# Products with a feature table for a few tiles per chunk, in a four-layer graph network on one core

## The chip, the cores and the metric

The kernel runs on one core of a Trainium2 chip. A core has five engines that run their own instruction streams side by side: TensorE (PE: matrix products, results in PSUM), VectorE (DVE), ScalarE (ACT), GpSimd (POOL) and SyncE (SP, which here only issues transfers). Sixteen DMA engines move data between memory and SBUF. The metric is the device time of one execution in microseconds (us), lower is better. Before the change the median of 14 runs is 22,172.26 us (22,068.88 to 22,297.55).

## What is computed

A graph of 12,500 nodes with 32 features and 400,000 edges sorted by target goes through four pre-norm residual layers. Each layer takes `h = relu(layernorm(x))`, makes a message per edge from the source's row (layer two from the target's row too) and adds the messages up at the targets. Cut to what matters here:

```python
# layer 0
m = relu(h[src] + edge_attr_32)
x = x + (1 + eps) * h + segment_sum(m, dst)
# layer 1: emb = edge_attr_10, edge_vec = edge_attr_3, norm = edge_weight
hid = sqrt(2) * relu(emb @ W1 / sqrt(10))
w = (hid @ W2 / 4).reshape(E, 7, 16, 8)
... # products of h[src], h[dst], directions and w; tanh gates
x = x + segment_sum(edge_ftr, dst)
# layer 2: rows are src, columns are dst
deg = segment_sum(ones, src); n = rsqrt(1 + deg)
xs = n * h
x = x + n * (segment_sum(xs[dst], src) + xs)
# layer 3: emb = edge_attr_8, edge_sh = edge_attr_4
hid = relu(emb @ (W1 / sqrt(8))) * sqrt(2)
w = (hid @ (W2 / 16)).reshape(E, 4, 8, 8)
... # products of h[src], edge_sh and w
x = x + segment_sum(edge_ftr, dst) / sqrt(E / N)
```

## The kernel before

Edges are cut into 196 chunks of CT = 16 tiles of 128 edges (2,048 edges a chunk); within a tile an edge is a partition. Everything is unrolled over the chunks. The stages follow one another: the first layer (`layer0`, run by `edges`), a joint pass over layers two and three (`edges12`), and the fourth layer (`edges3`). Between them `norm_relu` writes the normed features of all nodes to memory (`feats`).

**Gathers.** The rows `h[src]` come by indirect DMA on POOL, one per tile of 128 edges: L488 in the first layer, L759 in the joint pass, L1184 in the fourth. So each stage has 16 gathers a chunk, 3,136 in all.

**First layer.** Tiles go in groups of four (G = 4). `fetch` loads a chunk's indices, edge attributes and places (`load` L482 and L480, `places_of` L463; two buffers) and gathers four groups ahead, into six buffers. `main` adds the attributes (L615, DVE) and takes the relu (L616, ACT). `collect` builds a one-hot of each edge's place in its window of targets (L420, DVE, f32) and multiplies it with the messages on PE, all 16 tiles into one PSUM tile (L423, f32); the window's sum is copied (L426, ACT) and stored by SP (`put`, L448). `tail` also counts how often each node is a source: the index is split into two coordinates (L630 to L633), each becomes a one-hot (L637), and PE multiplies the two (L640, bf16). Beside all this a generator `rest` clears tables, makes weights, unit vectors and the bf16 parts of `edge_attr_8` for the fourth layer (`parts_of`, L313, 14 steps); `edges` draws from it after every second group (L563).

**Joint pass.** One pass of the loop (L993, 199 passes, 12 steps each) works on several chunks at once: the products of layer two for chunk c, its gather for c + 3, the front for c + 1, the sums for c - 1, and layer three for c - 3 and c - 4. `ends` (L773) turns the gathered rows over with 16 f32 products against the identity a chunk (L778), multiplies the window of targets with a one-hot (L782), and copies the tile X (L784, ACT). `hidden` (L794) makes the hidden layer, `product` (L801) and `reduce` (L811) the messages with an elementwise product z on DVE between them (L804). `collect` (L844) sums over targets. For layer three `lay` (L918) spreads target rows over edges, `alike` (L926) marks equal sources within a tile, `join` (L934) sums over them on PE and ACT copies the sum (L936), and `scatter` (L940) adds it to memory by an indirect DMA on POOL, 16 a chunk. PSUM tiles of the pool `ps` have one buffer.

**Fourth layer.** `edges3` multiplies hidden layer and weights in f32 (L1220) and uses a helper that the other stages don't: `thirds` (L429) writes an f32 tile as the sum of three bf16 tiles, so that a bf16 product with a one-hot keeps f32 accuracy.

## Time and profile before

| | us |
|---|---|
| median of 14 runs | 22,172.26 |
| the profiled execution | 22,128.07 |
| its span | 22,126.4 |
| first layer (first gather to the last sum stored) | about 120 to 5,140 |
| joint pass | about 5,250 to 16,500 |
| fourth layer | about 16,600 to 22,050 |
| PE busy | 14,400.2 (65%) |
| DVE busy | 11,884.2 (54%) |
| ACT busy | 5,787.4 (26%) |
| POOL busy | 14,365.1 (65%) |

Busy times are sums over the span; the stages have different limits, so each is read by itself, in a window of its own. A group of instructions in the profile is one line of the kernel, one engine and one operation: its names (written <- read), count, busy time and mean length, and then how long the engine stood idle before its instructions and what ended that. "Issue" there is time in which the engine waited for nothing that the profile shows. The column PEclk is the share of its full clock that TensorE was granted by the record. Timeline rows give the start, the length, the engine, the line and the operation.

### The profile page before, as it was taken

To read this page: it belongs to the slowest core of one execution; us is meant where nothing else is said; L and a number is where in the kernel's file an instruction comes from. 1 tells how busy PE (TensorE), PEld (TensorE's weight loads), DVE (VectorE), ACT (ScalarE), POOL (GpSimd) and SP (SyncE) were. 2 spreads that over 40 slices of the span, in tenths; PEclk is the share of its full clock that TensorE was granted. 3 is DMA by queue.
4 is the path that set the end of the run, shared out by engine and by line. 5 is a ranking of instruction groups with operands and counts; after the bars stand their busy time and mean duration, and the time that the engine had idled before them with its cause. 6 is when DMAs were issued, how large, how long until landed. Compare 5 with 4: busy or idle time off the path is not lost.

```text
span 22126.4 us, 218835 instructions
## 1 busy us (share of the span) xinstructions
PE 14400.2 (65%) x69780; PEld 8225.2 (37%) x69780; DVE 11884.2 (54%) x23464; ACT 5787.4 (26%) x13374; POOL 14365.1 (65%) x12552
## 2 busy tenths in 40 slices
PE   2333333334777777777777777777746777777776
PEld 2333333332332333333333333333325555555554
DVE  3444333334555555555555555555555666666666
ACT  0001000001222222222222222222214444444443
POOL 5666666664777777777777777777765555555554
PEclk9999999999777777777777777777768888888887
DMA  2114111112333333333333333333331111111111
GB/s 85 40 38 143 23 23 22 22 22 57 80 78 76 79 80 80 74 80 80 75 79 78 76 81 79 78 76 82 79 73 23 23 24 23 23 23 23 23 23 30
DMA packets 1528330, 1259.87 MB, mean 57 GB/s; under 512 B 1140160, under 2 KB 1303608, under 8 KB 1472776
## 3 DMA queue, kind: packets, MB, share of 16 engines
q1 hardware_dynamic: 741084, 1005.43, 14.6%
q0 software_dynamic: 752640, 206.32, 10.8%
q10 hardware_dynamic: 33430, 33.95, 0.5%
q8 instruction: 553, 9.06, 0.2%
q14 instruction: 623, 5.10, 0.1%
HBM read 1083.53 MB, written 160.90 MB: 56 GB/s over the span
## 4 chain that ended last, share of the span: by engine, by line
PE 31%; another core or an unknown queue 23%; DVE 18%; ACT 12%; issue 9%; POOL 4%; DMA 3%; DVEq 0%; ACTq 0%; SPq 0%; POOLq 0%
PE ps_y L801 11%; PE ps_o L811 5%; PE ps L934 4%; PE ps_w L1220 4%; ACT oh L836 4%; DVE z L804 3%; POOL hs L488 3%; ACT oh L765 2%; PE ps_win L423 1%; DVE pv L1228 1%; DVE pa L1224 1%; DVE f L1237 1%; PE ps_sum L844 1%; PE ps_m L778 1%
## 5 line engine op out<-in xcount | busy, mean ns | idle before, releaser
L940 POOL DMA_INDIRECT acc<-summed,rows x3136 | 4994.0, 1592 | 2052.2 <-issue 1132.9
L1184 POOL DMA_INDIRECT hs<-feat,src x3136 | 3030.8, 966 | 2455.7 <-DVE ps L1226 1457.0
L488 POOL DMA_INDIRECT hs<-feat,src x3136 | 3166.6, 1010 | 1963.1 <-issue 872.3
L759 POOL DMA_INDIRECT hs<-feat,src_c x3136 | 3172.8, 1012 | 1131.1 <-issue 936.8
L804 DVE TENSOR_TENSOR z<-ps_y,hid 128x1024 f32<-128x1024 f32 x2352 | 2843.7, 1218 | 1210.0 <-PE ps_y L801 957.8
L1220 PE MATMUL ps_w<-w2b,hid 128*128 128x256 f32 x12544 | 3208.2, 412 | 59.8 <-issue 39.9
L423 PE MATMUL ps_win<-m,oh 128*128 128x32 f32 x6272 | 1484.7, 402 | 2291.4 <-ACT m L616 1363.5
L1220 PEld LDWEIGHTS ps_w<-w2b,hid 128*128 128x128 f32 x12544 | 2593.1, 210 | 622.0 <-issue 82.7
L801 PE MATMUL ps_y<-X,w2t 64*128 64x512 f32 x4704 | 2238.0, 831 | 746.6 <-ACT hid L796 407.0
L423 PEld LDWEIGHTS ps_win<-m,oh 128*128 128x128 f32 x6272 | 1396.7, 328 | 2379.3 <-ACT m L616 1454.0
L811 PE MATMUL ps_o<-z,sums 128*32 128x512 f32 x9408 | 1924.6, 694 | 1.6 <-issue 0.8
L801 PE MATMUL ps_y<-Q,w2t 64*128 64x512 f32 x4704 | 1667.4, 733 | 79.7 <-DVE z L804 39.5
L934 PEld LDWEIGHTS ps<-hd,eq 128*128 128x128 f32 x6272 | 1044.1, 252 | 1265.0 <-issue 395.5
L934 PE MATMUL ps<-hd,eq 128*128 128x32 f32 x6272 | 1139.9, 335 | 544.5 <-DVE eq L926 189.2
L778 PE MATMUL ps_m<-eye,hs 128*32 128x128 f32 x6272 | 808.0, 369 | 1022.4 <-ACT X L784 740.1
L787 DVE TENSOR_TENSOR Q<-N,X 128x512 f32<-128x512 f32 x392 | 271.5, 693 | 2205.8 <-ACT X L784 1485.4
L1197 ACT ACTIVATE hid<-ps_h 128x1024 f32<-128x1024 f32 x784 | 800.8, 1021 | 2388.9 <-remote 1951.4
L1224 DVE TENSOR_TENSOR pa<-ps_w,q 128x512 f32<-128x512 f32 x784 | 538.4, 687 | 1648.6 <-remote 1353.5
L801 PEld LDWEIGHTS ps_y<-X,w2t 64*128 64x128 f32 x4704 | 600.3, 235 | 1795.4 <-issue 732.2
L778 PEld LDWEIGHTS ps_m<-eye,hs 128*32 128x32 f32 x6272 | 551.2, 148 | 1606.7 <-ACT X L784 866.2
L936 ACT COPY summed<-ps 128x128 f32<-128x128 f32 x784 | 207.8, 265 | 3584.5 <-PE ps L934 2368.8
L616 ACT ACTIVATE m<-m 128x128 f32<-128x128 f32 x784 | 241.9, 309 | 3417.5 <-DVE m L615 1644.4
(202 smaller groups left out, 20233.6 us busy)
## 6 DMA issues: line engine op xcount, KB each, us to landing
has<-loc_t SPq DMA_DIRECT2D x392, 1024.0 KB
srow<-in_src_t SPq DMA_DIRECT2D x392, 512.0 KB
hs<-feat,src POOLq DMA_INDIRECT x6272
N<-n_t SPq DMA_DIRECT2D x3136, 32.0 KB
emb<-pp SPq DMA_DIRECT2D x126, 448.0 KB
emb<-emb SPq DMA_DIRECT2D x196, 288.0 KB
edge_attr<-in_edge_attr SPq DMA_DIRECT2D x196, 256.0 KB
hs<-feat,src_c POOLq DMA_INDIRECT x3136
```

Of the source, the lines that this page charges most:

```text
L423: nc.tensor.matmul(c["sum"], lhsT=oh[:, k, :], rhs=feat[:, k, :], start=t0 + k == 0, stop=t0 + k == self.CT - 1)
L488: self.nc.gpsimd.indirect_dma_start(out=t[:, k, :], out_offset=None, in_=self.feats[l][:], in_offset=bass.IndirectOffsetOnAxis(ap=idx[:, t ...
L759: nc.gpsimd.indirect_dma_start(out=c["hs"][:, k, :], out_offset=None, in_=self.feats[1][:], in_offset=bass.IndirectOffsetOnAxis(ap=c["src_ ...
L778: nc.tensor.matmul(t[64 * q : 64 * q + 32, k * P : (k + 1) * P], lhsT=c["hs"][:, 4 * (2 * h + q) + k, :], rhs=self.eye, start=True, stop=True)
L801: nc.tensor.matmul(y[:, q, :], lhsT=self.w2t[64 * q : 64 * q + 64, j, :], rhs=c["Q" if j < 3 else "X"][64 * q : 64 * q + 64, h, :], start= ...
L804: nc.vector.tensor_mul(z, y, c["hid"][:, 2 * h : 2 * h + 2, :])
L811: nc.tensor.matmul(c["o", j // 3][32 * q : 32 * q + 32, :], lhsT=self.sums[:, j, :], rhs=c["z", j, q // 2][:, q % 2, :], start=j % 3 == 0, ...
L836: nc.scalar.activation(c["oh"][:, k, :], self.iota, AF.Square, bias=c["local"][:, k : k + 1], scale=-1.0)
L934: nc.tensor.matmul(t[:, k, :], lhsT=c["eq"][:, k, :], rhs=c["hd"][:, G * g + k, :], start=True, stop=True)
L940: nc.gpsimd.indirect_dma_start(out=self.tabs[2][k % NTAB][:], out_offset=bass.IndirectOffsetOnAxis(ap=c["rows"][:, G * g + k : G * g + k + ...
L1184: nc.gpsimd.indirect_dma_start(out=c["hs"][:, k, :], out_offset=None, in_=self.feats[3][:], in_offset=bass.IndirectOffsetOnAxis(ap=c["src" ...
L1220: nc.tensor.matmul(w[:, k, :], lhsT=c["hid"][:, m, 4 * g + k].rearrange("p q s -> p (q s)"), rhs=self.w2b[:, m, :], start=m == 0, stop=m == 1)
```

## The change

The last KP = 3 tiles of a chunk in the first layer, and the last KJ = 1 in the joint pass, are no longer gathered. A table of all features stands in SBUF as bf16 triples (`table`): 13 blocks of 128 rows, a row holding eight nodes, in two halves of 16 features. `codes` writes for each such edge the block, the place in the block and the node's number within the row. `found` turns these into one-hots, multiplies the table with them (13 x 2 x 3 products), keeps the one of eight nodes that is wanted, and folds the result into the tile of rows. The first three chunks (FIRST) gather all.

The first layer is written anew (`edges0`), chunk by chunk, with four buffers for loads and rows; the sums over targets go by thirds in bf16, with one-hots from ACT; the old form stays as `any0` for another kind of input that doesn't occur here. `rest` is drawn eight times a chunk, from chunk 4 on, and has more to do: `edge_attr_10` is split as `edge_attr_8` was, and each in 28 steps of half the size.

In the joint pass DVE transposes the rows (`sources`) in place of PE; the targets alone go by PE and are copied by ACT in four pieces (`targets`); the hidden layer reads the bf16 parts; the sums over targets and over equal sources go by thirds (`thirds`, `split`), the latter reduced by DVE (`joined`) where ACT copied before. Many tiles have one buffer instead of two. The fourth layer keeps its instructions.

```diff
+KP = 3
+KJ = 1
+FIRST = 3
+KB = 13
...
-        self.w1t = keep.tile([P, P], F32, name="w1tk")
-        self.w2t = keep.tile([P, 6, P], F32, name="w2t")
+        self.w1t = keep.tile([90, P], BF16, name="w1tk")
+        self.w2t = keep.tile([P, 2, 6, P], F32, name="w2t")
...
+            yield from self.parts_of(pool, self.a["ea10_c"], self.emb10)
             yield from self.parts_of(pool, self.a["ea8_c"], self.emb8)
...
-        F = flat.shape[1] // 14
+        F = flat.shape[1] // 28
...
+    def table(self, pool, l):
+        nc = self.nc
+        tab = pool.tile([P, 3, KB, 2, P], BF16, name="tab")
+        with self.tc.tile_pool(name="whole", bufs=1) as tmp:
+            x = tmp.tile([P, KB, 2 * P], F32, name="whole")
+            m = -(-self.N // 8)
+            rows = self.feats[l][: 8 * m].rearrange("(r k) d -> r (k d)", k=8)
+            n = m // P
+            nc.vector.memset(x[:, n:, :], 0.0)
+            nc.sync.dma_start(x[:, :n, :], rows[: n * P].rearrange("(b p) e -> p b e", p=P))
+            nc.sync.dma_start(x[: m - n * P, n, :], rows[n * P :])
+            for k in range(3):
+                for i in range(2):
+                    nc.scalar.copy(tab[:, k, :, i].rearrange("p b (j f) -> p b j f", f=16),
+                                   x.rearrange("p b (j i f) -> p b i j f", i=2, f=16)[:, :, i])
+                if k < 2:
+                    for i in range(2):
+                        t = x.rearrange("p b (j i f) -> p b i j f", i=2, f=16)[:, :, i]
+                        nc.vector.tensor_tensor(t, t, tab[:, k, :, i].rearrange("p b (j f) -> p b j f", f=16), op=ALU.subtract)
+        return tab
+    def edges0(self, rest):
+        nc, tc, CT, NW = self.nc, self.tc, self.CT, self.NW
+        n = KP * P
+        self.codes()
+        with ExitStack() as ctx:
+            tp = ctx.enter_context(tc.tile_pool(name="table0", bufs=1))
+            tab = self.table(tp, 0)
...
+            def fetch(c):
+                c["src"] = self.load(ld, "src", c["col"])
+                c["attr"] = self.load(ld, "edge_attr_32", c["col"])
+                c.update(self.places_of(ld, c["no"]))
+                if c["no"] >= FIRST:
+                    c["code"] = ld.tile([P, 3, n], F32, name="code", bufs=3)
+                    nc.sync.dma_start(c["code"].rearrange("p i e -> p (i e)"),
+                                      self.code[c["no"] : c["no"] + 1].rearrange("o i e -> (o i e)").partition_broadcast(P))
+                c["hs"] = ld.tile([P, CT, D], F32, name="hs")
+                for k in range(CT if c["no"] < FIRST else CT - KP):
+                    nc.gpsimd.indirect_dma_start(
+                        out=c["hs"][:, k, :], out_offset=None, in_=self.feats[0][:],
+                        in_offset=bass.IndirectOffsetOnAxis(ap=c["src"][:, k : k + 1], axis=0))
+            def found(c, step):
+                if c["no"] < FIRST:
+                    return
+                if step == 0:
+                    c["mine"] = wp.tile([P, n], BF16, name="mine")
+                    nc.vector.scalar_tensor_tensor(c["mine"], c["code"][:, 1], self.part, c["code"][:, 0],
+                                                   op0=ALU.is_equal, op1=ALU.mult)
+                    c["found"] = [pt.tile([P, n], F32, name=f"ps_half{i}") for i in range(2)]
+                elif step < 6:
+                    for b in range(3 * (step - 1), min(3 * step, KB)):
+                        oh = wp.tile([P, n], BF16, name="oh8", bufs=4)
+                        nc.vector.tensor_scalar(oh, c["mine"], float(b + 1), None, op0=ALU.is_equal)
+                        for i in range(2):
+                            for k in range(3):
+                                nc.tensor.matmul(c["found"][i], lhsT=tab[:, k, b, i], rhs=oh,
+                                                 start=(b, k) == (0, 0), stop=(b, k) == (KB - 1, 2))
+                else:
+                    own = []
+                    for i in range(2):
+                        own.append(wp.tile([P, n], F32, name=f"own{i}"))
+                        nc.vector.scalar_tensor_tensor(own[i], c["code"][:, 2], self.quad, c["found"][i],
+                                                       op0=ALU.is_equal, op1=ALU.mult)
+                    t = po.tile([P, KP, D], F32, name="ps_own")
+                    for k in range(KP):
+                        for i in range(2):
+                            nc.tensor.matmul(t[:, k, :], lhsT=own[i][:, k * P : (k + 1) * P], rhs=self.fold2[:, i],
+                                             start=i == 0, stop=i == 1)
+                    nc.scalar.copy(c["hs"][:, CT - KP :, :], t)
+            def messages(c):
+                m = c["f"] = wp.tile([P, CT, D], F32, name="m")
+                nc.vector.tensor_add(m, c["hs"], c["attr"])
+                nc.scalar.activation(m, m, AF.Relu)
+            def places(c, g):
+                oh = c["oh", g] = wp.tile([P, G, P], BF16, name="oh", bufs=2 * CG)
+                for k in range(G):
+                    t = G * g + k
+                    nc.scalar.activation(oh[:, k, :], self.iota, AF.Square, bias=c["local"][:, t : t + 1], scale=-1.0)
+                nc.scalar.activation(oh, oh, AF.Relu, bias=self.one, scale=-2.0)
+            def collect(c, g):
+                if g == 0:
+                    c["sum"] = ps.tile([P, B], F32, name="ps_sum")
+                for k in range(G * g, G * g + G):
+                    nc.tensor.matmul(c["sum"][: 3 * D, 0:P], lhsT=c["f3"][:, k].rearrange("p i f -> p (i f)"),
+                                     rhs=c["oh", g][:, k % G, :], start=k == 0, stop=k == CT - 1)
...
+            cs = [{"no": c, "col": c * CT} for c in range(NW)]
+            for c in range(2):
+                fetch(cs[c])
+            for c in range(NW + 1):
+                now, last, next_ = (cs[k] if 0 <= k < NW else None for k in (c, c - 1, c + 1))
+                if c + 2 < NW:
+                    fetch(cs[c + 2])
+                for g in range(CG):
+                    if now:
+                        if g == 0:
+                            messages(now)
+                            now["deg"] = ps.tile([P, P], F32, name="ps_deg")
+                            now["hl"] = self.coordinates(wp, now["src"])
+                        self.thirds(wp, now, g, bufs=2)
+                        places(now, g)
+                        hi, lo = now["hl"]
+                        self.degree(wp, now, hi[:, G * g : G * g + G], lo[:, G * g : G * g + G], G * g)
+                    if next_:
+                        for step in ((0, 1), (2, 3), (4, 5), (6,))[g]:
+                            found(next_, step)
+                    if last:
+                        if g < 2:
+                            collect(last, 2 * g)
+                            collect(last, 2 * g + 1)
+                        else:
+                            add(last, g - 2)
+                    for _ in range(2 if c > 3 else 0):
+                        next(rest, None)
+            for _ in rest:
+                pass
...
+            tab = self.table(ctx.enter_context(tc.tile_pool(name="table1", bufs=1)), 1)
...
-                c["emb"] = ld.tile([P, B], F32, name="emb")
-                for q in range(Q4):
-                    nc.sync.dma_start(c["emb"][32 * q : 32 * q + 10],
-                                      self.a["ea10_c"][q, :, ds(row, 1), :].rearrange("f o e -> f (o e)"))
+                c["emb"] = ld.tile([90, Q4 * B], BF16, name="emb")
+                nc.sync.dma_start(c["emb"], self.emb10[:, :, ds(row, 1), :].rearrange("k f o e -> (k f) (o e)"))
...
+                    c["src"] = gp.tile([P, CT], I32, name="src", bufs=12)
+                    nc.sync.dma_start(c["src"], self.a["src"][:, ds(c["col"], CT)])
                     c["hs"] = gp.tile([P, CT, D], F32, name="hs")
-                for k in range(G * g, G * g + G):
+                    if c["no"] >= FIRST:
+                        c["code"] = gp.tile([P, 3, KJ * P], F32, name="code", bufs=2)
+                        for i in range(3):
+                            nc.sync.dma_start(c["code"][:, i], self.code[c["no"], i, (KP - KJ) * P :].partition_broadcast(P))
+                for k in range(G * g, min(G * g + G, CT - (KJ if c["no"] >= FIRST else 0))):
                     nc.gpsimd.indirect_dma_start(
                         out=c["hs"][:, k, :], out_offset=None, in_=self.feats[1][:],
-                        in_offset=bass.IndirectOffsetOnAxis(ap=c["src_c"][:, k : k + 1], axis=0))
+                        in_offset=bass.IndirectOffsetOnAxis(ap=c["src"][:, k : k + 1], axis=0))
...
+            def found(c, s):
...
+                elif s in (1, 2):
+                    for b in ((0, 1, 2, 3, 4, 5, 6), (7, 8, 9, 10, 11, 12))[s - 1]:
+                        nc.vector.tensor_scalar(c["which"][:, b], c["mine"], float(b + 1), None, op0=ALU.is_equal)
+                if s in (2, 5):
+                    c["half"] = ps.tile([P, B], F32, name="ps_2")[:, :n]
...
+                elif s in (3, 6):
...
+                elif s == 8:
...
-            def ends(c, h):
+            def sources(c, h):
+                nc.vector.transpose(c["X"][:, h, :], c["hs"].rearrange("p t f -> p (t f)"))
+
+            def targets(c):
                 t = ps.tile([P, B], F32, name="ps_m")
-                for k in range(4):
-                    for q in range(2):
-                        nc.tensor.matmul(t[64 * q : 64 * q + 32, k * P : (k + 1) * P],
-                                         lhsT=c["hs"][:, 4 * (2 * h + q) + k, :], rhs=self.eye, start=True, stop=True)
-                for q in range(2):
-                    e0 = (2 * h + q) * B
-                    nc.tensor.matmul(t[64 * q + 32 : 64 * q + 64, :], lhsT=c["win"], rhs=c["has"][:, e0 : e0 + B],
+                for g in range(Q4):
+                    b = g ^ 1
+                    nc.tensor.matmul(t[32 * g : 32 * g + 32, :], lhsT=c["win"], rhs=c["has"][:, b * B : (b + 1) * B],
                                      start=True, stop=True)
-                nc.scalar.copy(c["X"][:, h, :], t)
+                for g in (1, 3, 0, 2):
+                    nc.scalar.copy(c["X"][32 * g : 32 * g + 32, (g ^ 1) % 2, :], t[32 * g : 32 * g + 32, :])
...
-                    r = 32 * (2 * h + q)
-                    nc.tensor.matmul(t[:, q, :], lhsT=self.w1t[r : r + 10], rhs=c["emb"][r : r + 10],
-                                     start=True, stop=True)
+                    e0 = (2 * q + h) * B
+                    nc.tensor.matmul(t[:, q, :], lhsT=self.w1t, rhs=c["emb"][:, e0 : e0 + B], start=True, stop=True)
...
-                    c["has2"] = sp.tile([P, Q4 * B], F32, name="has2")
+                    c["has2"] = sp.tile([P, Q4 * B], F32, name="has2", bufs=1)
...
+            def split(c, step):
+                if step == 0:
+                    c["hd3"] = sp.tile([P, CT, 3, D], BF16, name="hd3", bufs=1)
+                if step % 2 == 0:
+                    nc.scalar.copy(c["hd3"][:, :, step // 2, :], c["hd"])
+                elif step == 1:
+                    nc.vector.tensor_tensor(c["hd"], c["hd"], c["hd3"][:, :, 0, :], op=ALU.subtract)
+                else:
+                    nc.vector.tensor_tensor(c["hd3"][:, :, 2, :], c["hd"], c["hd3"][:, :, 1, :], op=ALU.subtract)
...
             def join(c, g):
-                t = ps.tile([P, B], F32, name="ps_2")[:, : G * D].rearrange("p (k f) -> p k f", f=D)
+                t = c["joint"] = ps.tile([P, B], F32, name="ps_2")[:, : G * 3 * D].rearrange("p (k e) -> p k e", k=G)
                 for k in range(G):
-                    nc.tensor.matmul(t[:, k, :], lhsT=c["eq"][:, k, :], rhs=c["hd"][:, G * g + k, :], start=True, stop=True)
+                    nc.tensor.matmul(t[:, k, :], lhsT=c["eq", g][:, k, :],
+                                     rhs=c["hd3"][:, G * g + k].rearrange("p i f -> p (i f)"), start=True, stop=True)
+
+            def joined(c, g):
                 c["summed", g] = sp.tile([P, G, D], F32, name="summed", bufs=2 * CG)
-                nc.scalar.copy(c["summed", g], t)
+                nc.vector.tensor_reduce(c["summed", g], c["joint"].rearrange("p k (i f) -> p k f i", i=3), AX.X, ALU.add)
...
```

## The prediction, made before the changed kernel was run

> **What bounds the kernel now.** I read the table of windows first, one row for the body of each stage: the first layer, the joint pass over the second and third layers, the fourth layer.
>
> ```profile
> core 0: us, PE busy (x) PEld busy (x) DVE busy (x) ACT busy (x) POOL busy (x), PEclk, DMA share, GB/s
> 2700.00:4900.00 2200.00, 796.36 (x4124) 755.97 (x4123) 794.40 (x2840) 119.19 (x430) 1362.92 (x1376) 1.00 0.12 22
> 5500.00:16300.00 10800.00, 8458.62 (x41536) 3312.97 (x41533) 6050.16 (x11835) 2871.56 (x6656) 7912.79 (x6076) 0.76 0.37 79
> 17000.00:21500.00 4500.00, 3240.82 (x14685) 2561.40 (x14683) 2904.03 (x3750) 2076.61 (x4564) 2523.16 (x2608) 0.84 0.12 23
> ```
>
> There are 196 chunks of 16 tiles. 1376 gathers in 2200 us are 86 chunks: 25.6 us per chunk in the first layer. The joint pass takes 11,250 us for its 199 passes of the loop, 56.5 us each, and the fourth layer some 27 us a chunk. In the first layer only POOL is more than half busy (62%); in the joint pass PE is (78%), with POOL beside it.
>
> Next the groups of instructions by line, of the window 2700 to 4900 and then of the whole span.
>
> ```profile
> L488 POOL DMA_INDIRECT hs<-feat,src x1376 | 1362.9, 990 | 829.2 <-issue 382.7 <-DVE oh L420 296.3 <-DMA src<-in_src 95.8
> ```
>
> ```profile
> L940 POOL DMA_INDIRECT acc<-summed,rows x3136 | 4994.0, 1592 | 2052.2 <-issue 1132.9
> L488 POOL DMA_INDIRECT hs<-feat,src x3136 | 3166.6, 1010 | 1963.1 <-issue 872.3
> L759 POOL DMA_INDIRECT hs<-feat,src_c x3136 | 3172.8, 1012 | 1131.1 <-issue 936.8
> ...
> L423 PE MATMUL ps_win<-m,oh 128*128 128x32 f32 x6272 | 1484.7, 402 | 2291.4 <-ACT m L616 1363.5
> ...
> L934 PE MATMUL ps<-hd,eq 128*128 128x32 f32 x6272 | 1139.9, 335 | 544.5 <-DVE eq L926 189.2
> L778 PE MATMUL ps_m<-eye,hs 128*32 128x128 f32 x6272 | 808.0, 369 | 1022.4 <-ACT X L784 740.1
> ```
>
> "Issue" on POOL is time between two of its DMAs in which it waits for nothing shown. In the first layer POOL needs (1362.9 + 382.7) / 86 = 20.3 us a chunk of its own; the other 5.3 us of the 25.6 it waits for buffers that DVE frees late. So fewer gathers help there, down to what the other engines allow. In the joint pass POOL needs (4994.0 + 1132.9 + 3172.8 + 936.8) / 196 = 52 us by this reckoning, or 49 us with the usual 1.25 us (gather) and 1.84 us (scatter) from start to start in the timeline. It then waits for sums from PE, while PE, 44 us busy a chunk, waits 740.1 us in all (3.8 us a chunk) for the copy of X before its transposes. PE's round with ACT and DVE sets the joint pass; POOL is 4 to 7 us behind it.
>
> **Clock.** The row of 2700 to 4900 says 1.00, but this is not to be trusted: L423 and L934 have one shape, and L423 costs 237 ns of PE time, L934 182. In the trace starts in L423 lie 210 ns apart; in L934 they lie either 110 or 210 apart. The 512-column bf16 product of the fourth layer (L1195) has starts 220 or 430 ns apart. I read the first layer as running at half clock, since its PE is busy 36% of the time, and price its PE work both ways.
>
> **First layer.** Removed: 3 of 16 gathers in all chunks but three. POOL: 20.3 x 13/16 = 16.5 us a chunk. Added on PE: 78 bf16 products (13 blocks x 2 halves x 3 parts) over 384 columns. From L1195, 220 x 384/512 = 165 ns or 322 ns: 12.9 us or 25.1. Six f32 products to fold the halves are 12 instructions of 110 or 210 ns: 1.3 or 2.5. The places' sums turn from 32 f32 instructions into 16 bf16 ones and the degrees stay: 32 x 60 (L1256 dense) or 110 ns, 1.9 or 3.5. PE: 16.3 us at full clock, 31.2 at half, against 9.3 now. DVE: 13 one-hots of 384 bf16 have no equal in this trace; between the small operations (150 ns) and the 128x384 f32 form (552 ns) they cost 2 to 7 us, and I take 3.5, nearer the small ones as they read and write bf16 with a scalar (the 128x2048 f32 form with a scalar, L768, 1.29 us, makes 0.24 for 384). With messages 0.7, thirds 1.4, degree one-hots 5.0, coordinates 0.7, halves 1.1 and the rest 0.4 it has some 13 us, against 9.2 now. The places' one-hots move to ACT: 16 x 0.39 + 4 x 0.71 = 9.1 us, 12 in all; that lies beside. SP carries as many DMAs as before with one 590 KB broadcast more; the put of the sums comes behind the loads of the chunk two ahead, but these now have four buffers in place of two.
>
> Nothing but POOL and PE is near the bound. What speaks against the one-hots is this:
>
> ```profile
> 9002.96 1.54 POOL L940 DMA_INDIRECT acc<-summed,rows  x1 [0.30 <-issue]
> ...
> 9004.29 1.28 DVE L768 TENSOR_SCALAR has<-has,part 128x2048 f32<-128x2048 f32 x1
> ...
> 9004.81 2.17 POOL L940 DMA_INDIRECT acc<-summed,rows  x1 [0.30 <-issue]
> ```
>
> In this timeline a POOL DMA that starts inside that operation takes 2.17 us and not 1.54. The Trainium skill, "SBUF — State Buffer", section "Who interferes with whom", says why: a DVE operation with a scalar in a two-port mode takes the ports that POOL shares, and POOL blocks for its whole length. By that rule all 13 one-hots a chunk could hold POOL up; by the row alone only one that meets a DMA's start does. I allow 2 us of the 3.5: POOL 18.5 us.
>
> A chunk then takes at least 18.5 us with PE at full clock. Of the 5.3 us of waiting I keep about half, 2.5, since whole-chunk buffers (four) replace six groups of four tiles: 21.0 us. Bounds: 17.5 (no wait, half the collisions) and 32 (half clock). (21.0 - 25.6) x 193 = -888 us.
>
> **The work beside it.** Edge attributes of layer two are now split into bf16 parts as well: 16 MB in and 72 MB out on top of 13 and 58, in 56 steps, drawn 8 a chunk and not 2. 159 MB at the 355 GB/s of the busiest slices of the present splitting are 448 us, in about 21 chunks (440 us at 21 us), with single-buffered parts that must be stored before the next step. A step is 8 us of DMA and some 4 us of copy and landing, 2.7 steps a chunk: 32 us in place of 21. I take +200 us (0 to +340).
>
> **Tables.** Twice 13 blocks of features are loaded, split by 6 ACT copies of 1664 columns (1.7 us each by the 1792-column cast) and 4 DVE subtractions (2.0 us by the 1792-column row), in a line between the stages, plus the codes: 60 + 45 us. Nothing hides them: +105 (70 to 180).
>
> **Joint pass.** PE loses 32 transposes (808.0 / 196 = 4.1 us) and with them the wait for X of 3.8; the sum over equal sources falls from 5.8 us (1139.9 / 196) to 16 bf16 products over 96 columns, about 1.5; the hidden layer (512.1 us, 2.6) to about 1.4. It gains 78 products over 128 columns at 60 or 110 ns, 4.7 or 8.6, at the stage's clock of 0.76 about 6.2, and 0.9 for the fold. Sum: -4.1 - 4.3 - 1.2 + 7.1 = -2.5 us of work. DVE rises from 32 us (6050 / 191 chunks) to about 41: two transposes 1.4, 13 one-hots 2.5, two halves and a code 0.7, splitting twice 2.8, four reductions over 96 columns each 2.3 in place of ACT's copies. It lies beside POOL's 49, but DVE's queue also holds the 12 products z that PE waits for, so each operation in between can hold PE 0.7 us. One PSUM bank (ps_2) now passes eight times a chunk between PE and DVE or ACT, five times before; three more hand-offs at 0.6 to 1 us cost 2 to 3 us, of which the X wait that goes (3.8) pays. Single buffers make a writer wait for the chunk before; by the steps of the loop each reader is done one step earlier at least, so I price them at nothing; the cost is 0.5 us apiece if not. POOL loses one gather, 1.25 us. I take -2.5 us: 54.0 us x 199 = -498 us. Bounds: 50.5 (POOL's 48.2 and half the present lag) to 60.
>
> **Fourth layer.** Same instructions, same buffers: 0.
>
> **Sum** against the profiled execution (22,128 us, span 22,126): -888 + 200 + 105 - 498 = -1,081, so 21,047. The median of the runs is 44 us above that execution: 21,090 us.
>
> **Rivals.**
> A. POOL sets both stages and the rest hides. For it: POOL is the busiest engine of the first layer, and DVE and ACT have room. Against: 5 to 7 us a chunk in which POOL waits in every stage. 17.5 and 50.5 us: -1,563 - 1,194 + 305, 19,720 us.
> B. Slower: the first layer's PE stays at half clock. It is one mechanism, the clock falling whenever PE idles: windows of 5 us in the fourth layer show 0.50 after a pause of PE and 1.00 in dense stretches, and the first layer has pauses of 10 us and more. 31.2 us of PE plus 1.5: +7.1 x 193 = +1,370 + 305 - 498, 23,350 us. It decides from 26.6 us a chunk on, PE's mean clock below about 0.62 of full. Against: 78 products in a row are dense, unlike today's bursts of 8, and dense stretches show full clock. The Trainium skill, "TensorE: Matmul & The Clock Gate", section "Part 1: The HAM clock gate", lets one busy window of some 3.4 us restore full clock; by that page each chunk would lose only an estimated 1.7 us, which no row of the first layer shows.
> C. The joint pass is lengthened: DVE's 41 us and the shared bank stand between PE's products, +4 us a chunk. For it: DVE waits most for PE and PE for ACT and DVE there, a round without slack. +796 - 888 + 305: 22,390 us.
> D. The first layer's time isn't POOL's at all; the stall of 5.3 us grows by what the gathers lose. Only the joint pass gains: 22,128 + 305 - 498 + 44 = 21,980 us.
>
> **How the numbers follow.** Forecast 0.55 (its own range 20,400 to 21,800), A 0.15, B 0.14, C 0.11, D 0.05. A measurement of this kernel can tell 0.3%, 66 us. Faster: the forecast, A, most of D and a little of C, 0.76. Same: 0.04, from C and D. Slower: B and most of C, 0.20. The range reaches over D and part of A and C: 20,000 to 22,350.
>
> **What would show it.** First layer: POOL's own need 16 to 19 us a chunk and a pitch of 21; the 384-column products 165 ns apart; longer gathers where a one-hot runs. Joint pass: the wait for X gone, PE near 41 us a chunk, a pitch of 54. The splitting: chunks of 30 us early in the first layer. I am wrong if the 384-column products lie 320 ns apart throughout, or if PE's waits for ps_2 exceed 4 us a chunk.

## The result, and the profile after

The changed kernel takes 23,293.54 us (median of 10 runs, 23,261.58 to 23,347.08), the kernel before 22,179.05 in the same comparison: a ratio of 1.050, with a 95% interval of 1.048 to 1.052. It is slower, where 21,090 was forecast. The profiled execution took 23,331.77 us (its span is 23,330.0). I cut both traces into stages:

| stage, us | before | after | change | forecast |
|---|---|---|---|---|
| start to the first gather of the first layer | 69 | 168 | +99 | +105 (with the second table) |
| first layer, to the last sum of degrees | 5,074 | 5,358 | +284 | -688 |
| of it: chunk, chunks 60 to 180 | 25.62 | 26.10 | +0.48 | 21.0 |
| of it: chunk, chunks 4 to 44 (beside the splitting) | 26.07 | 31.79 | +5.7 | some 30 |
| between them, to the first product z of the joint pass | 193 | 231 | +38 | (in the +105) |
| joint pass, to the first gather of the fourth layer | 11,247 | 12,001 | +755 | -498 |
| of it: one pass of the loop | 56.85 | 61.36 | +4.5 | 54.0 |
| fourth layer and end | 5,542 | 5,571 | +28 | 0 |

The chunk lengths of the first layer in this table are distances between the sums of degrees on DVE, one a chunk. Both kernels here give the same by their stored window sums, the last step of a chunk (25.50 and 26.10 for chunks 60 to 180). In kernels without the first layer's table the degrees run ahead of the messages, so for those I count by the stored sums of chunks 84 to 180, behind the end of the splitting (about chunk 40 at the changed kernel's pace, 73 at half of it); by that measure before has 25.36 and after 26.08.

The windows of the changed kernel over the bodies of the three stages (busy time and, in brackets, instructions of each engine; then granted clock, DMA share and GB/s):

```profile
core 0: us, PE busy (x) PEld busy (x) DVE busy (x) ACT busy (x) POOL busy (x), PEclk, DMA share, GB/s
1000.00:5000.00 4000.00, 3154.36 (x18412) 1962.21 (x18411) 1823.54 (x4831) 1542.62 (x3942) 2004.05 (x1968) 0.79 0.24 69
6000.00:17000.00 11000.00, 8180.61 (x42055) 2892.79 (x42054) 6863.15 (x15941) 3241.60 (x6879) 7298.84 (x5588) 0.76 0.38 81
18200.00:22700.00 4500.00, 3215.36 (x14569) 2537.11 (x14567) 2886.17 (x3725) 2062.83 (x4536) 2506.21 (x2597) 0.84 0.12 23
```

In the first layer POOL fell from 62% to 50% busy, as three gathers fewer must make it, and PE rose from 36% to 79%. In the joint pass PE's share fell from 78% to 74% and POOL's from 73% to 66%, while the pass got longer: nobody is at a bound there. The fourth layer is as it was. The groups of the whole span (mean duration in ns, then idle time ahead of the group and what ended most of it):

```profile
L1186 POOL DMA_INDIRECT acc<-summed,rows x3136 | 5111.8, 1630 | 3097.0 <-DVE far L1171 1785.6
...
L752 POOL DMA_INDIRECT hs<-feat,src x2557 | 2611.3, 1021 | 2848.5 <-DVE m L788 1487.1
L1031 DVE TENSOR_TENSOR z<-ps_y,hid 128x1024 f32<-128x1024 f32 x2352 | 2832.6, 1218 | 2410.6 <-remote 1408.3
L771 PE MATMUL ps_half<-oh,tab 128*128 128x384 bf16 x15054 | 3250.4, 368 | 792.6 <-issue 534.0
```

Both POOL groups now wait for DVE. In the first layer, window 2700 to 4900 (84 chunks):

```profile
POOL hs L752 <- DVE m L788: 786.2, 84, 10.4
...
ACT oh L795 <- PE ps_half L771: 587.5, 77, 12.6
...
ACT oh L795 <- remote: 368.0, 32, 12.7
```

And DVE, at its costliest operation, waits 1,408.3 us for "remote". The page uses that word where no recorded instruction of the core ends at the moment of release. This kernel has one core, so nothing is remote. I took each recorded event of PE's semaphore in the trace and looked for the last matmul before it that raises it (its end is modelled by the profile): in these waits the matmul had ended, and its signal came up to 16 us late in the joint pass. Signals of DVE are not over 2 us late there. The first layer of the kernel before shows the same, in its waits (total us, how many, longest):

```profile
engine line waited for: us in total, times, longest us
...
ACT wsum L426 <- remote: 591.4, 33, 23.0
DVE deg L643 <- remote: 442.6, 27, 28.9
...
POOL hs L488 <- issue: 382.7, 1250, 2.1
```

That is the window 2700 to 4900 which the prediction used; these two lines stood in the waits of that window, and I did not follow them up. ACT and DVE together stood there for 12 us a chunk (1,034 / 86) waiting for finished matmuls. That it is the signal and not the matmul that is late is seen in the timeline:

```profile
3028.60 1.91 PE L423 MATMUL ps_win<-m,oh 128*128 128x32 f32 x8
3030.32 0.64 PE L640 MATMUL ps_deg<-olo,ohi 128*125 128x100 bf16 x4
3050.86 0.18 ACT L426 COPY wsum<-ps_win 128x32 f32<-128x32 f32 x1 [22.32 <-remote]
```

The first line holds the last products of a chunk's sum. PE goes on to four matmuls for the degrees, and the copy of the sum starts 20 us after them.

### The profile page after: what moved, and what is told of

Read it like the earlier page. It is cut to its first block, busy times and chain, and to the rows that moved or that the text cites. A ratio compares the mean times of both kernels' runs of the same rounds, so it can differ in the third digit from the quotient of the medians.

```text
span 23330.0 us, 262444 instructions
## 1 busy us (share of the span) xinstructions
PE 16767.3 (72%) x86904; PEld 8736.8 (37%) x86904; DVE 13635.6 (58%) x28376; ACT 8081.1 (35%) x18170; POOL 13576.9 (58%) x11780
## 4 chain that ended last, share of the span: by engine, by line
PE 45%; DVE 21%; another core or an unknown queue 16%; issue 10%; ACT 5%; DMA 2%; POOL 1%; ACTq 0%; SPq 0%; DVEq 0%; POOLq 0%
PE ps_half L771 12%; PE ps_y L1028 8%; PE ps_o L1038 7%; DVE z L1031 5%; PE ps_w L1485 4%; PE ps L978 4%; PE ps_own L782 2%; PE ps L1143 2%; DVE pv L1493 1%; PE ps L1177 1%; DVE f L1502 1%; DVE pa L1489 1%; ACT oh L1063 1%; DVE eq L1163 1%
## 5 line engine op out<-in xcount | busy, mean ns | idle before, releaser
L1449 POOL DMA_INDIRECT hs<-feat,src x3136 | 3028.1, 966 | 2488.1 <-DVE ps L1491 1489.0
L752 POOL DMA_INDIRECT hs<-feat,src x2557 | 2611.3, 1021 | 2848.5 <-DVE m L788 1487.1
L1031 DVE TENSOR_TENSOR z<-ps_y,hid 128x1024 f32<-128x1024 f32 x2352 | 2832.6, 1218 | 2410.6 <-remote 1408.3
L771 PE MATMUL ps_half<-oh,tab 128*128 128x384 bf16 x15054 | 3250.4, 368 | 792.6 <-issue 534.0
L1028 PE MATMUL ps_y<-Q,w2t 64*128 64x512 f32 x4704 | 2366.8, 854 | 1927.2 <-DVE z L1031 975.4
L955 POOL DMA_INDIRECT hs<-feat,src x2943 | 2824.8, 960 | 1160.9 <-issue 916.5
L771 PEld LDWEIGHTS <-tab 128*128 128x128 bf16 x15054 | 1592.4, 110 | 2153.6 <-issue 1508.5
L1028 PEld LDWEIGHTS ps_y<-Q,w2t 64*128 64x128 f32 x4704 | 610.5, 239 | 3099.8 <-DVE z L1031 1574.2
L1028 PE MATMUL ps_y<-X,w2t 64*128 64x512 f32 x4704 | 1666.4, 634 | 121.4 <-DVE z L1031 85.2
L795 ACT ACTIVATE oh<-iota,local 128x128 bf16<-128x128 f32 x3136 | 1019.2, 390 | 2049.6 <-PE ps_half L771 1057.7
L768 DVE TENSOR_SCALAR oh<-mine 128x384 bf16<-128x384 bf16 x2509 | 620.7, 268 | 1869.1 <-PE ps_half L771 1169.2
L1460 PE MATMUL ps_h<-emb,w1s 72*128 72x512 bf16 x1568 | 554.1, 440 | 834.0 <-ACT hid L1462 388.1
L978 PE MATMUL ps<-which,tab 128*128 128x128 bf16 x15054 | 1014.3, 232 | 185.1 <-DMA hs<-feat,src 104.7
L978 PEld LDWEIGHTS <-tab 128*128 128x128 bf16 x15054 | 947.6, 105 | 524.2 <-issue 515.7
L1063 ACT ACTIVATE oh<-iota,local 128x128 bf16<-128x128 f32 x3136 | 996.9, 390 | 268.0 <-PE ps_sum L1070 207.5
```

The source lines that it names most:

```text
L752: nc.gpsimd.indirect_dma_start(out=c["hs"][:, k, :], out_offset=None, in_=self.feats[0][:], in_offset=bass.IndirectOffsetOnAxis(ap=c["src" ...
L771: nc.tensor.matmul(c["found"][i], lhsT=tab[:, k, b, i], rhs=oh, start=(b, k) == (0, 0), stop=(b, k) == (KB - 1, 2))
L795: nc.scalar.activation(oh[:, k, :], self.iota, AF.Square, bias=c["local"][:, t : t + 1], scale=-1.0)
L955: nc.gpsimd.indirect_dma_start(out=c["hs"][:, k, :], out_offset=None, in_=self.feats[1][:], in_offset=bass.IndirectOffsetOnAxis(ap=c["src" ...
L978: nc.tensor.matmul(c["half"], lhsT=tab[:, k, b, i], rhs=c["which"][:, b], start=(b, k) == (0, 0), stop=(b, k) == (KB - 1, 2))
L1028: nc.tensor.matmul(y[:, q, :], lhsT=self.w2t[64 * q : 64 * q + 64, h, j, :], rhs=c["Q" if j < 3 else "X"][64 * q : 64 * q + 64, h, :], sta ...
```

## The experiments

Where no median is named, a time is that of one profiled execution. The runs met four chips, on which the kernel before took 22,106 (e1 to e4), 22,148 (e5 to e8), 21,820 (e9 to e12) and 21,809 to 21,863 us (e13 to e18). Across chips I compare chunks and passes rather than totals, and keep 1.5% in mind.

### e1 and e2: the first layer without its table, and with one tile

e1 sets the number of tiles by table to 0 in the first layer (no table there, all 16 tiles gathered); e2 sets it to 1.

```diff
-KP = 3
+KP = 1        # e2; e1: 0 in the first layer, the joint pass as it was
```

> First layer without its table: all 16 tiles gathered, the rest of the rewritten layer kept; joint pass as changed. Theory (PE's 78 products of 384 columns, 17 us of PE busy a chunk, set the first layer): a steady chunk falls from 26.1 us to what POOL's 16 gathers need, 20 to 22 us, the stage by some 900 us. Rival (the rewritten loop, its hand-offs or ACT's one-hots set it): the chunk stays within 1 us of 26. The joint pass stays at 61 us a pass under both.

> First layer with one tile by the table instead of three: the 78 products are 128 columns wide, 5 to 9 us of PE instead of 17; 15 gathers. Theory (PE's products set the first layer): a chunk near POOL's need, 19 to 21 us. Rival (each of the 13 one-hots with its hand-off between DVE and PE costs the same whatever the width): 24 to 26 us.

Measured: e1 23,002.79 us, chunk 24.93 (stored sums; the degrees, running ahead, give 23.95); e2 23,567.28, chunk 27.48. With no table the first layer is 1.15 us a chunk faster than with three tiles (26.08), so the table loses where it was meant to gain; but it does not fall to the 20 to 22 us that POOL needs. And one tile, with products a third as wide, is worse than three: the width of the products isn't all. Chunks 4 to 44 stayed long, 28.92 and 31.90 (30.78 in the changed kernel), so most of that belongs to the splitting beside them and not to the table.

### e3, e4, e5, e6: the joint pass

e3 leaves out table and products in the joint pass. e4 issues the loads of a later chunk at step 6 of the loop in place of step 0. e5 keeps the joint pass's turns at bank ps_2 but does 6 of the 78 products. e6 keeps all the work and moves the products and the fold to bank ps_m.

```diff
 # e5
-                    for b in range(KB):
+                    for b in range(1):
 # e6
-                    c["half"] = ps.tile([P, B], F32, name="ps_2")[:, :n]
+                    c["half"] = ps.tile([P, B], F32, name="ps_m")[:, :n]
...
-                    t = ps.tile([P, B], F32, name="ps_2")[:, : KJ * D].rearrange("p (k f) -> p k f", f=D)
+                    t = ps.tile([P, B], F32, name="ps_m")[:, : KJ * D].rearrange("p (k f) -> p k f", f=D)
```

> Joint pass without its table (16 gathers, no found), all else as changed. Theory (single buffers and the shifted order of loads made the pass 4.4 us longer, the products only little of it): still 58 to 61 us a pass. Rival (the products with the table, 5.2 us of PE busy a chunk, their DVE work and their turns in the shared PSUM bank make it): 55 to 57 us, as before the change or better. First layer unchanged at 26 us.

> Joint pass with the loads for the chunk after next (22 DMAs, 16 of them for N) issued at step 6 of the pass instead of at its start. In the changed kernel they fall beside the gathers and the first two products, before which DVE waits 10.5 us a pass. Theory (PE's results come late while these loads and the gathers run together): the wait moves or shrinks, the pass falls to 52 to 57 us. Rival (the wait belongs to these two products wherever the loads stand): the pass stays at 60 to 62 us.

> Joint pass with its table, but of the 78 products per chunk only the 6 of the first block are made (the found row is right only for nodes of that block; one-hots, loads, bank turns, folding and the missing 16th gather all stay). Theory (the products themselves, 5.2 us of PE busy a pass, lengthen PE's round): 53 to 56 us a pass, against 61.4 with all and 52.2 without the table. Rival (DVE's one-hots and hand-offs, the loads and the bank turns do it): 58 to 61 us.

> Joint pass with its table, where found's products use the PSUM bank of the transposes' place (ps_m, once a pass) instead of ps_2, which the sums over equal sources and the spread rows use. Theory (turns in ps_2 hold PE and DVE up): 55 to 58 us a pass. Rival (the bank is free in time anyway): 60 to 62 us.

| | total, us | pass, us |
|---|---|---|
| after | 23,330 | 61.36 |
| e3 no products | 21,643.72 | 52.22 |
| e4 loads later | 22,949.58 | 58.92 |
| e5 6 of 78 products, bank ps_2 | 23,031.96 | 59.62 |
| e6 all products, bank ps_m | 21,640.56 | 52.02 |

Two words in the code are worth 9.3 us a pass and 1,690 us in all, more than either expectation for e6 allowed. The work of the products is not the loss: with 6 of them the pass is still 59.62, with all 78 in another bank 52.02. Where the time went is seen in DVE's waits, window 8000 to 12000, of after and of e6 (L1031 there is L1032 here, L1182 is L1183):

```profile
DVE z L1031 <- remote: 529.9, 98, 12.8
DVE summed L1182 <- PE ps L1177: 328.8, 129, 4.6
DVE z L1031 <- issue: 296.5, 126, 9.9
```

```profile
DVE summed L1183 <- remote: 406.1, 72, 15.1
DVE z L1032 <- PE ps_y L1029: 223.0, 212, 4.9
DVE summed L1183 <- PE ps L1178: 170.5, 109, 8.2
DVE z L1032 <- remote: 56.4, 29, 6.8
```

In after, z waits 8.1 us a pass (529.9 over 65.2 passes) for late signals. z is in the middle of the round: PE needs it for the reductions, and the last z frees the bank for the next product. In e6 the late signals meet the sums of equal rows instead (406.1 us), which POOL needs only later, and z is left with 56.4. So the wrong bank costs this much because the order that its turns force puts z's products under the late signals. That the bank is the cause is shown by e3, e5 and e6; that the order is how it acts is read from the waits. That the loads' place matters too (e4, 2.4 us a pass) fits it, as the loads decide when the gathers start.

With the bank moved, POOL is the bound of the joint pass: in e6 its busy and issue time are 3,867 of 4,000 us (3,212.6 + 341.1 + 313.8). Without the joint table it waits for nothing at all, as in e8, whose pass is 52.53 (window 8000 to 12000):

```profile
L1184 POOL DMA_INDIRECT acc<-summed,rows x1222 | 2014.1, 1648 | 372.5 <-issue 342.0 <-DVE z L1029 13.1 <-DVE Q L1013 4.0
L953 POOL DMA_INDIRECT hs<-feat,src x1216 | 1244.9, 1024 | 370.7 <-issue 367.0 <-DMA hs<-feat,src 3.7
```

Busy and issue time are 3,968 of 4,000 us.

### e7 and e8: more one-hot buffers; no tables at all

e7 gives the first layer's one-hots 13 buffers in place of 4; its joint pass has no products, and two buffers for the large one-hots that after holds once. e8 has no table in either stage, the same double buffers, and draws 4 pieces of the splitting a chunk in place of 8.

```diff
 # e7
-                        oh = wp.tile([P, n], BF16, name="oh8", bufs=4)
+                        oh = wp.tile([P, n], BF16, name="oh8", bufs=13)
 # e8
-                    for _ in range(2 if c > 3 else 0):
+                    for _ in range((2 if g % 2 else 0) if c > 3 else 0):
```

> Two stages changed. First layer with all 13 one-hots of a chunk buffered (four before), three tiles by the table: theory (a one-hot waits until PE frees a buffer, and holds DVE's queue and then PE): the steady chunk falls from 26.1 to 20 to 24 us; rival (PE's products at their mixed clock set it): 25 to 27 us. Joint pass without the table and with two buffers for the places' one-hots and for the spread one-hots: if single buffers cost anything, below 51 us a pass; if POOL sets the pass, 51.5 to 52.7, as with single buffers (52.2).

> No table in either stage, the rest of the change kept, two buffers for the two kinds of one-hots, and the work beside the first layer drawn 4 a chunk instead of 8. Theory (both tables are losses, the rest of the change is a gain, the early chunks of the first layer are slowed by the drawn work): early chunks 24 to 27 us instead of 32, steady 24, joint pass 52: 20,800 to 21,200 us, faster than both kernels. Rival (the drawn work only moves its delay to later chunks): the first layer still ends after 5,050 us, 21,250 us or more.

Measured: e7 21,717.78 us, first layer's chunk 25.69, pass 52.63; e8 21,298.91, chunk 25.19 (stored sums), pass 52.53. Free one-hot buffers are worth 0.4 us a chunk, not the 5 that are missing. Double buffers for the two large one-hots of the joint pass bring nothing (52.63 against e3's 52.22), so single ones cost nothing there. In e8 the second case of the expectation came: chunks 4 to 44 take 24.67 us, but chunks 44 to 84, beside which the splitting now runs on, take 28.53, and the first layer ends at 5,139 us. From first gather to last stored sum it takes 5,053 us, the kernel before 5,071: without a table the rewritten first layer gains next to nothing, and e8's gain is the joint pass's.

### e9: the whole change with bank and pace mended

The edits of e6 and, for the splitting, of e8; both tables stay.

> The whole change, both tables and all products kept, with two small edits: the joint pass's products and fold use bank ps_m, as in e6, and the first layer draws 4 pieces of the rest's work a chunk in place of 8. If the bank and the pace are two separate losses, their gains add: joint pass 52.0 us, chunks 4 to 44 down from 31.7 to about 26.5, steady chunks after the 84th still at 26.1, total 21,640 - 200 = 21,440 (21,350 to 21,540). If the early chunks are long for another reason (the table's first use, a clock not yet raised), they stay above 30 and the total stays at 21,600 to 21,700.

Measured: 21,247.97 us; pass 51.65, chunks 4 to 44 26.10 and 60 to 180 26.04 (by the stored sums 27.02 for 44 to 84, and 25.74 from 84 on). The two losses are separate, and both go, the second but for one us in chunks 44 to 84. On this chip the kernel before takes 21,820.04, so the whole change with these few words altered is 2.6% faster than before, in one execution. What is still missing is the first layer.

### e10, e11, e12: what keeps the first layer's chunk at 26 us

e10 multiplies one of the table's three parts. e11 is e8 with three buffers of gathered rows in place of four. e12 is e8 with every use of PE's results in the first layer moved about a chunk later.

```diff
 # e10, first layer
-                            for k in range(3):
+                            for k in range(1):
 # e11
-                c["hs"] = ld.tile([P, CT, D], F32, name="hs")
+                c["hs"] = ld.tile([P, CT, D], F32, name="hs", bufs=3)
 # e12
-            ps = ctx.enter_context(tc.tile_pool(name="ps0", bufs=2, space=PSUM))
+            ps = ctx.enter_context(tc.tile_pool(name="ps0", bufs=4, space=PSUM))
...
-                        else:
-                            add(last, g - 2)
+                        if g == 3:
+                            nc.vector.tensor_add(self.deg, self.deg, last["deg"][:NP, : self.J])
+                    if old and g < 2:
+                        add(old, g)
```

> e9 with one of the three bf16 pieces of the table multiplied in the first layer (26 products a chunk in place of 78): the rows found there are the reference's to bf16 precision alone. One-hots, found, fold, copies and waits are the same in number. If TensorE's work sets the first layer's chunk, its busy time falls by two thirds of the 16.8 us that L771 holds a chunk, some 11 us, and the chunk falls from 26.1 to 23.95 (e1's) or less, down to some 21; total 20,700 to 21,150 where e9 gives 21,440. If the hand-offs between one-hots, products and fold set it, the chunk stays at 25.5 or more and the total within 100 us of e9's.

> e8 (no tables, slow rest) with 3 buffers for the rows that POOL gathers in the first layer in place of 4, so that POOL can run one chunk less ahead. If TensorE's completion signals wait for POOL to pause, the stalls get shorter with the run-ahead: the longest waits of ACT and DVE for it fall from the 43 to 70 us of e8 to under 50, and the chunk moves little from 24.4 (23.5 to 25.5), total 21,150 to 21,500. If the signals are late by a time of their own, the waits keep their length, and with less slack POOL stands longer: chunk 26 or more, total above 21,550.

> e8 with every use of a TensorE result in the first layer moved later: the degree sum added a chunk later, the window sum copied and folded a chunk later, four banks each for both, six buffers for the degree one-hots. Joint pass as in e8 (52.5). If the signals are late by up to some 40 us whatever POOL does, nothing waits for them any more and the chunk falls to POOL's own 16 x 1.31 us = 21.0: total 21,300 - 150 x 3.4 = 20,790 (20,700 to 20,900). If they come only when POOL pauses, the stalls come more rarely and last longer, and the chunk falls less, to 23 to 24.4: total 21,080 to 21,300. Against the kernel before the ratio would be 0.94 or 0.955.

Measured: e10 20,815.57 us, chunk 24.15 (by the stored sums 23.77); e11 21,084.96, chunk 24.57; e12 21,114.11 (median of 4), ratio 0.968 (0.966 to 0.971), chunk 24.30 (these two by the stored sums). PE's work does count: 52 products fewer take 1.9 us off the chunk. It is then a little below the kernels without any table on the same chip, and still far above POOL's need of 17 us for 13 gathers. Moving the uses a chunk later didn't help as a fixed lateness would have it: the waits became longer (55 of DVE's for the degrees, the longest 61.9 us, in window 1000 to 5000; e8 had 41, the longest 42.5). A shorter run ahead (e11) changed the lengths little and in both directions (longest 37.1 to 54.2 us, 36.5 to 70.1 in e8); it doesn't tell the two apart.

### e13 and e14: the first layer without gathers

A plain load of as many rows takes the place of the indirect ones, in e9 (three tiles by table) and in the same kernel without the first layer's table.

```diff
-                for k in range(CT if c["no"] < FIRST else CT - KP):
-                    nc.gpsimd.indirect_dma_start(
-                        out=c["hs"][:, k, :], out_offset=None, in_=self.feats[0][:],
-                        in_offset=bass.IndirectOffsetOnAxis(ap=c["src"][:, k : k + 1], axis=0))
+                n_own = CT if c["no"] < FIRST else CT - KP
+                nc.sync.dma_start(c["hs"][:, :n_own, :], self.feats[0][: P * n_own].rearrange("(p t) d -> p t d", p=P))
```

> e9 with the first layer's 13 gathers a chunk replaced by one plain load of as many rows (always the same rows, so the messages are not the reference's): POOL is still there, all else is as in e9, whose chunk is 26.04 us with TensorE busy for 21.5 of it. If TensorE's work alone sets the chunk, POOL's rest changes nothing: 25 to 26 us, total 21,050 to 21,300 on a chip like e9's. If the chunk is TensorE's work and on top of it stalls that come from POOL's gathers (signals of TensorE held until POOL pauses), it falls to TensorE's own 21 to 22.5 and the total to 20,450 to 20,700; signals of TensorE that come over 2 us late disappear.

> The first layer without tables and without gathers (one plain load of 16 tiles' rows a chunk, always the same, so the messages are not the reference's), the joint pass as in e9. In e8 a chunk is 24.4 us, of which ACT is busy 9.7, DVE 8.5, TensorE 4.4 and POOL's gathers take 21. If the held signals come from the gathers, they are gone, and with POOL's 21 us gone too the chunk falls to 10 to 15 us: total 18,700 to 19,500. If TensorE's signals are late whatever POOL does, by the 20 to 40 us of e8 and e12, the stalls of DVE and ACT stay and the chunk stays at 19 us or more: total above 20,000.

Measured: e13 19,321.23 us, chunk 15.95; e14 18,170.84, chunk 9.11 (stored sums; the degrees run up to 40 chunks ahead and give 7.05). e13 fell far below what either theory gave. e14's first layer ends at 2,237 us, 11.4 a chunk over the whole of it, within the 10 to 15 of the first theory, and its total is below that theory's. The windows of e9 (2000 to 3000 and 3000 to 4000) and of e13:

```profile
2000.00:3000.00 1000.00, 789.27 (x4691) 504.44 (x4689) 459.11 (x1230) 391.42 (x1001) 521.67 (x514) 0.78 0.23 65
3000.00:4000.00 1000.00, 824.58 (x4808) 529.05 (x4807) 455.37 (x1240) 387.64 (x1010) 505.77 (x503) 0.79 0.16 44
```

```profile
2000.00:3000.00 1000.00, 1000.00 (x7781) 693.30 (x7780) 708.09 (x2004) 621.14 (x1629) 0.00 (x0) 1.00 0.22 70
```

PE is busy all the time at clock 1.00 and does 7,781 matmuls where e9 did 4,691. So PE sets e13's chunk, at the 16 us of work that the prediction reckoned at full clock, and the 26.04 us of e9 are 10.1 more: by e9's steady row 3000 to 4000 (PE 824.58 of 1,000 us busy, so 21.5 of the 26.04) 4.6 us of pauses, and 5.5 us because PE's own work takes 21.5 and not 15.95. The starts of the 384-column products show some of the second part: 163 ns in the median of both, but in e9 1,105 of 6,078 lie 300 to 345 apart (half clock), in e13 37 of 9,640. At 159 ns each and 77 chunks that is 2.3 of the 5.5 us. The groups of e13 in that window name what is waited for, and "remote" is not among it:

```profile
L770 PE MATMUL ps_half<-oh,tab 128*128 128x384 bf16 x4895 | 836.7, 326 | 0.0
...
L794 ACT ACTIVATE oh<-iota,local 128x128 bf16<-128x128 f32 x1001 | 324.6, 389 | 124.4 <-PE ps_sum L801 124.4
L767 DVE TENSOR_SCALAR oh<-mine 128x384 bf16<-128x384 bf16 x815 | 197.3, 255 | 200.7 <-PE ps_half L770 200.7
```

In e14 ACT sets the pace: it is busy 1,020.31 of 1,100 us.

```profile
700.00:1800.00 1100.00, 552.78 (x4078) 523.50 (x4079) 970.86 (x2213) 1020.31 (x2688) 0.00 (x0) 1.00 0.50 163
```

PE's recorded signals, counted in the traces of the first layer:

```
kernel   window        signals   over 2 us late   their sum, us   longest, us
before   2500 to 4500      400              156           1,966          30.8
after    2500 to 4500    1,670              193             559           5.2
e8       2500 to 4500      363              116           1,758          47.9
e12      2500 to 4500      203               87           2,578          61.6
e9       2500 to 4500    1,654              101             332           5.1
e10      2500 to 4500    1,147              210             909          12.2
e13       500 to 3000    3,367                0               0           0.0
e14       500 to 1800      819                0               0           0.0
```

Without gathers, none of 4,186 signals is late. Traffic isn't the reason: e14's window 700 to 1800 moves 163 GB/s, e9's above 65. Nor is the number of packets: e13 has 54 a us between 1500 and 3000, 30 of them under 512 bytes, after has 44 and 26 between 2500 and 4500. It is POOL's gathers that delay PE's signals; that they do so in the kernel before, whose gathers no run took away, is concluded from the same late signals there. PE is not quite alone: of ACT's own signals 25 of 684 are over 2 us late in e12's window (longest 6.5), and none of 3,924 in e13 and e14.

### e15: the version meant to beat both

No table in the first layer, e12's later uses there, the joint pass with its one tile's products in bank ps_m.

> No table in the first layer, the later uses of e12 there, and the joint pass with its one tile's products in bank ps_m as in e9. If the parts add, the first layer is e12's (23.9 us a chunk) and the joint pass e9's 51.65 where e12 has 52.41: total 21,100 - 200 x 0.76 = 20,950 (20,850 to 21,050) on a chip like that of e9 and e12, ratio 0.960 (0.955 to 0.966). If the table's products in the joint pass bring nothing and e9's 51.65 was its chip alone, the total is 21,100 and the ratio e12's 0.968.

Measured: 20,981.74 us (median of 4), ratio 0.960 (0.956 to 0.964); chunk 24.39 (stored sums), pass 51.53. The joint pass's table is worth something after all: on the chip of e9 to e12 the pass is 51.65 and 51.64 with it, 52.41 and 52.41 without (e11, e12), 0.8 us a pass and some 150 us in all, about 60% of the gather that it saves (1.3 us).

### e16, e17, e18: can the gathers be kept and the delay lost?

e16 puts a small fill on POOL after every fourth gather of e9. e17 releases e9's gathers in groups of four by a copy on DVE, five groups ahead; e18 does so six groups ahead, with no table in the first layer.

```diff
 # e16
+                    if k % 4 == 3:
+                        nc.gpsimd.memset(c["tick"], 0.0)
 # e17, at each of a chunk's four steps
+                    gathers(4 * c + g + 5)
...
+                nc.vector.tensor_copy(c["idx"][:, j], c["src"][:, j])
+                for k in range(j.start, j.stop):
+                    nc.gpsimd.indirect_dma_start(
+                        out=c["hs"][:, k, :], out_offset=None, in_=self.feats[0][:],
+                        in_offset=bass.IndirectOffsetOnAxis(ap=c["idx"][:, k : k + 1], axis=0))
```

> e9 (chunk 26.04 us, POOL's own need 13 x 1.31 = 17) with one small fill of 64 words a partition on POOL after every fourth gather, which nothing reads. If another instruction of POOL between the gathers lets TensorE's signals through, they are late by no more than four gathers, some 5 us, the stalls shrink and the chunk falls below 24; total under 20,850 on a chip like e9's. If the signals wait for POOL to stand still, or the four gathers are enough to hold them, the chunk stays at 25.5 to 26.5, total 21,150 to 21,400.

> e9 with the first layer's gathers released in groups of four by VectorE (a small copy of their row numbers at each of a chunk's four steps), five groups ahead, so that POOL stands still between groups whenever VectorE is behind. If signals held until POOL pauses are what keeps the chunk at 26.0 us, a stall can't outlast the few gathers released, TensorE stays at full clock more of the time, and the chunk falls to 18 to 23 us (without gathers it was 15.95): total 20,000 to 20,650, ratio 0.92 to 0.945. If lateness goes by the number of gathers, not by how they are bunched, or if POOL now waits as much as the others did, the chunk is 25 to 28: total 21,050 to 21,650, ratio 0.965 to 0.99.

> As e17, six groups ahead, with no table in the first layer (16 gathers a chunk, POOL's own need 21.0 us; e15, which has the later uses of the sums in its place, has 23.87). If the bunching makes the stalls, the chunk falls to 21.5 to 23: total 20,500 to 20,800 on a chip like e15's, ratio 0.94 to 0.952. If it doesn't, or POOL's new waits cost what the stalls did, 24 to 25.5: total 20,990 to 21,300, ratio 0.96 to 0.975.

Measured: e16 21,256.71 us, chunk 25.83; e17 21,182.91 (median of 4), ratio 0.971 (0.969 to 0.974), chunk 26.27; e18 20,944.06 (median of 4), ratio 0.961 (0.958 to 0.963), chunk 24.71 (stored sums), which is the second theory's; its total lies between the two. Neither an instruction between the gathers nor their release in groups removes the delay with the table: 145 and 160 late signals of 1,660 and 1,674 (e16, e17), 437 and 478 us, against e9's 101 and 332. Without the table the groups give nothing either: e18's first layer, from first gather to last stored sum, takes 4,947 us, e15's 4,963, and the two can't be told apart (intervals 0.956 to 0.964 and 0.958 to 0.963). Both beat before by 4% and after by more. My reading that long runs of gathers without a pause make the delay is not borne out.

## Why the prediction was wrong

**First layer: "of the 5.3 us of waiting I keep about half ... 21.0 us".** This is the first step that failed; the chunk is 26.10, and the stage 972 us above the forecast. The 5.3 us were called buffers that DVE frees late, and I took half of them to be cured by larger buffers; POOL's wait for DVE grew to 9.4 us a chunk instead (786.2 / 84). What DVE and ACT were late for was not asked. It was signals of PE delayed by the gathers, and PE's own products: with the gathers gone the chunk is 15.95 (e13), and with two thirds of the products gone 24.15 (e10). POOL's own 16.5 us a chunk was right (POOL busy and issue time, 1,096.74 + 307.8 us for 84 chunks, are 16.7) and decided nothing.

**PE's work at full clock, 16.3 us.** Right as work: 15.95 in e13 (the terms of the prediction add up to 16.1). In after it is 21.3 (1,798.44 of 2,200 us busy, times 26.1). The half-clock starts are 977 of 5,986 between products, 12.8 a chunk, or 2.0 us at 159 ns each, of the 5 us; what the rest is stays open. The Trainium skill, "TensorE: Matmul & The Clock Gate", section "Part 1: The HAM clock gate", was cited with an estimate of 1.7 us a chunk by one window of some 3.4 us: for these products the trace agrees, with 12.8 slow starts, some 4 us of half clock a chunk. Products lay 163 ns apart, as forecast (165), not 320.

**The one-hots' collisions with POOL, 2 us a chunk.** Not seen: gathers take 1,002 ns in the window 2700 to 4900 (1,096.74 / 1,094), 990 before, which is 0.2 us a chunk. The Trainium skill, "SBUF — State Buffer", section "Who interferes with whom", lets VectorE operations in a two-port mode block POOL; for these one-hots of 268 ns no run here shows it. DVE's 13 one-hots took 3.5 us (13 x 268 ns), as I chose.

**The splitting, +200 us.** Right: 40 chunks at 5.7 us above the later ones are 228 (188 by the stored sums); drawing it at half the pace takes most of it away (e9).

**Tables, +105 us.** Right in size: 99 at the start and 38 between the stages, 137 in a range of 70 to 180.

**Joint pass: "three more hand-offs at 0.6 to 1 us cost 2 to 3 us, of which the X wait that goes (3.8) pays".** The second step that failed, and the larger: 61.36 for 54.0, the stage 1,253 us above the forecast. The resource was named, and its price, which had no row behind it, was wrong. The bank cost 9.3 us a pass (61.36 against e6's 52.02), since a turn that is lost isn't one hand-off: it moves what stands in PE's order behind it to another time, here under the gathers. The rest of the sum held and was even too small: with the bank out of the way the pass is 52.02 and not 54.0. All of the joint pass's edits together then bring 4.8 us against before's 56.85, and POOL's reckoned 52 is what they meet. Single buffers at nothing: right for the two that e7 doubled.

**Fourth layer, 0.** Measured +28 us.

**The rivals.** B gave 23,350 and hit the number by accident: its first layer stood at 32.7 us, on half clock throughout, and its joint pass at 54.0; measured are 26.1, with a clock of 0.80, and 61.4. C had the joint pass right, place, resource and size (+4 for a measured +4.5), with too small a chance and with the first layer's gain left in. D was right that the first layer isn't POOL's. What happened is C and D together: 22,128 + 796 + 305 + 44 make 23,273. I had no case in which both of the change's halves failed; the range ended at 22,350.

## What to carry to other kernels

A wait that the profile cannot put down to an instruction of the core is a question to be answered before a gain is forecast there: on one core, "remote" meant finished work whose signal came late, and no buffer count cured it. A PSUM bank that another step of a pipelined loop shares is priced not by its hand-offs but by what the forced order moves, so give a new step a bank whose turns lie apart from the loop's round, and try that first. When a change has parts in several stages, forecast the case in which two of them fail, and measure them apart: here the same diff held a gain of 4.8 us a pass, a loss of 9.3 and a table that cost about 1.2 us a chunk. And count a stage by its last step: the sums of degrees ran ahead, and by them the kernels without a table looked faster than they were.
